# A selective scan with its row multiply moved to DVE and sums by identity matmuls, and an attention that normalises on GpSimd and transposes

## The chip, the cores and the metric

The kernel runs on one core of one Trainium2 chip. The engines are TensorE (PE for its matmuls, PEld for its weight loads), VectorE (DVE), ScalarE (ACT), GpSimd (POOL) and SyncE (SP), which here only starts DMAs. They run side by side and wait for each other through semaphores. The metric is the device time of one execution in microseconds (us); smaller is better. Everything is fp32.

## The reference

Eight images of 384 channels and 1024 positions pass a first layer (two Mamba scans, forward and backward, and a depthwise convolution), and then attention; five of the images have a feed-forward layer after it. What matters here, cut down:

```
def mamba(x, ...):
    ...
    delta = softplus(dt @ dt_proj_w.T + dt_proj_b)         # (b, l, 384)
    A = -exp(A_log)                                        # (384, 16)
    deltaA = exp(delta[..., None] * A)
    deltaBu = (delta * u)[..., None] * Bm[:, :, None, :]   # 16 states per channel
    def step(h, inp):
        dA, dBu, c = inp
        h = dA * h + dBu
        return h, einsum('bdn,bn->bd', h, c)               # summed over the 16 states
    _, ys = scan(step, h0, (deltaA, deltaBu, Cm))
    y = ys + u * D_param
    return (y * silu(z)) @ out_proj_w.T
...
scores = einsum('bhqd,bhkd->bhqk', q, k)                   # 6 heads, 1024 positions
attn = softmax(where(causal, scores, -inf))
out = einsum('bhqk,bhkd->bhqd', attn, v)
return out.reshape(B, T, 384) @ Wproj + bproj
```

## The kernel before, in words

Channels lie on partitions: 384 channels are NC = 3 chunks `c` of 128, and the 1024 positions lie along the free dimension, in NH = 2 halves of 512[...], or NT = 8 blocks of 128. The outer loop goes over the images b; one image runs `layer0`, `attention` and, for the first five, `feed_forward`.

In `layer0` the inputs are projected, convolved and passed through softplus into `u` (input), `dl` (delta) and `bcv` (the 16 B rows and 16 C rows, on 32 partitions), each for two directions d. L337 to L339 end the softplus, L370 turns `u` into `u*dl` on POOL. The two `bcv` go out to DRAM (L347).

The scan loops over d, over the n = 16 states and over the three chunks c:

- L377: a DMA reads a B row and a C row from DRAM and spreads each over 128 partitions (`brow`, `crow`; two buffers each).
- L385: POOL multiplies g = u*dl times brow, 128x1024, into one of six g buffers.
- L390: ACT makes the decays, da = exp(delta*A), 128x512, in PSUM.
- L396 (d = 0) or L399 (d = 1, reversed): DVE runs the recurrence over 512 positions, twice per c, the second half starting from the first one's last column.
- L402: POOL multiplies g by crow, in place.
- L404: PE adds eight transposes of g into `y` in PSUM, so that y gathers the sum over n and d with positions on partitions. L362 has put u times D there first.

After the scan ACT copies y to SBUF (L416), PE transposes it back (L424), DVE multiplies it by the gate `sz` (L428), and the output projection follows (L434, L441).

In `attention`, queries are worked on in blocks of 128: a head has two groups g of QT = 4 blocks. `probabilities` computes the scores of a block against the n = 128 to 1024 keys up to it (L502), adds the mask (L509), takes the row maximum (L513), the exponential with its row sum (L515) and the reciprocal (L516); L517 then makes on POOL a 128x128 diagonal matrix `dg` of the reciprocals. `weighted_values` turns every 128x128 block of probabilities by a matmul with dg as its moving operand (L529), which normalises it as well; DVE copies the result to SBUF (L537) and PE multiplies it by the values (L538). The loop calls `probabilities` of one group ahead of `weighted_values` of the group before it.

A framework inserts the semaphore waits and orders each engine's instructions by priority and its own estimate of times, so the order on an engine isn't that of the source; each engine then works through its queue in order. Buffers with the same tag are reused in turn: a write waits for the last reader of the buffer it takes.

Of the kernel before, what the change touches and what calls it, by code (L numbers as in the profile page):

```python
# [8 lines left out]
F32 = mybir.dt.float32  # L9
AF = mybir.ActivationFunctionType  # L10
ALU = mybir.AluOpType
AX = mybir.AxisListType
PSUM = bass.MemoryType.PSUM

P = 128
B, C, H, W = 8, 384, 32, 32
L = H * W
NC = C // P
HB = 512
NH = L // HB  # L20
NT = L // P
NS = 16
# [10 lines left out]
FFN_B = GROUPS * (B // GROUPS)  # L33
QT = HB // P
MASKED = -1e30
NR = 1


V_NORM, V_CW, V_CB, V_DTB, V_D, V_DW, V_DWB, V_BP, V_B2, V_ALOG = 0, 1, 5, 6, 7, 8, 17, 18, 19, 20
# [4 lines left out]
def kernel(  # L44
# [16 lines left out]
    nc = tc.nc  # L61
# [1 line left out]
    const = ctx.enter_context(tc.tile_pool(name="const", bufs=1))  # L63
    xpool = ctx.enter_context(tc.tile_pool(name="xpool", bufs=1))
    tpool = ctx.enter_context(tc.tile_pool(name="tpool", bufs=1))
    dpool = ctx.enter_context(tc.tile_pool(name="dpool", bufs=2, space=bass.MemoryType.DRAM))

    def ctile(name, shape):
        return const.tile(shape, F32, name=name, tag=name)
# [31 lines left out]
    ident = ctile("ident", [P, P])  # L101
# [9 lines left out]
    amat = ctile("amat", [P, NC, NS])  # L111
    nc.scalar.activation(amat, vec[:, :, V_ALOG : V_ALOG + NS], AF.Exp)
    nc.vector.tensor_scalar(amat, amat, -1.0, None, ALU.mult)
    diagd = ctile("diagd", [P, NC, P])
# [83 lines left out]
    def layer0(b, xt):  # L198
        t = tpool.tile([P, NC, L], F32, name=f"t_{b}", tag="t")
        with tc.tile_pool(name=f"l0_{b}", bufs=1) as lp:  # L200
# [140 lines left out]
                        )  # L341


            drows = []
            for d in range(2):
                dr = dpool.tile([2 * NS, L], F32, name=f"dr{d}_{b}", tag=f"dr{d}")
                nc.sync.dma_start(out=dr, in_=bcs[d])  # L347
                drows.append(dr)

            with tc.tile_pool(name=f"scan_{b}", bufs=2) as sp:
              with tc.tile_pool(
                name=f"yps_{b}", bufs=1, space=PSUM
              ) as yps, tc.tile_pool(name=f"scanps_{b}", bufs=2, space=PSUM) as ps:
                y = yps.tile([P, NC, NT, P], F32, name=f"y_{b}", tag="y")
                for d in range(2):
                    u, dl = us[d], dls[d]
                    for c in range(NC):  # L360
                        for j in range(NT):
                            nc.tensor.matmul(  # L362
                                out=y[:, c, j, :],
                                lhsT=u[:, c, j * P : (j + 1) * P],
                                rhs=diagd[:, c, :],
                                start=(d == 0 and j % 4 == 0),
                                stop=False,
                                skip_group_check=True,
                            )
                        nc.gpsimd.tensor_tensor(u[:, c, :], u[:, c, :], dl[:, c, :], ALU.mult)  # L370
                    for n in range(NS):
                        if n % NR == 0:
                            rows_bc = []
                            for which in range(2):
                                s = which * NS + n
                                rt = sp.tile([P, NR, L], F32, name=f"bc{which}_{d}_{b}_{n}", tag=f"bc{which}")
                                nc.sync.dma_start(  # L377
                                    out=rt,
                                    in_=drows[d][s : s + NR, :].unsqueeze(0).to_broadcast([P, NR, L]),
                                )  # L380
                                rows_bc.append(rt)
                        brow, crow = (rt[:, n % NR, :] for rt in rows_bc)
                        for c in range(NC):
                            g = sp.tile([P, L], F32, name=f"g_{d}_{b}_{n}_{c}", tag="g", bufs=6)
                            nc.gpsimd.tensor_tensor(g, u[:, c, :], brow, ALU.mult)  # L385
                            for i in range(NH):
                                h = i if d == 0 else NH - 1 - i
                                lo, hi = h * HB, (h + 1) * HB
                                da = ps.tile([P, HB], F32, name=f"da_{d}_{b}_{n}_{c}_{h}", tag="da")
                                nc.scalar.activation(  # L390
                                    da, dl[:, c, lo:hi], AF.Exp, scale=amat[:, c, n : n + 1]
                                )
                                gh = g[:, lo:hi]
                                if d == 0:
                                    first = 0.0 if i == 0 else g[:, lo - 1 : lo]
                                    nc.vector.tensor_tensor_scan(gh, da, gh, first, ALU.mult, ALU.add)  # L396
                                else:
                                    first = 0.0 if i == 0 else g[:, hi : hi + 1]
                                    nc.vector.tensor_tensor_scan(  # L399
                                        gh[:, ::-1], da[:, ::-1], gh[:, ::-1], first, ALU.mult, ALU.add  # L400
                                    )
                            nc.gpsimd.tensor_tensor(g, g, crow, ALU.mult)  # L402
                            for j in range(NT):
                                nc.tensor.matmul(  # L404
                                    out=y[:, c, j, :],
                                    lhsT=g[:, j * P : (j + 1) * P],
                                    rhs=ident,
                                    is_transpose=True,
                                    start=False,
                                    stop=(d == 1 and n == NS - 1),  # L410
                                    skip_group_check=True,
                                )

                yt = us[0].rearrange("p c (j k) -> p c j k", k=P)
                for c in range(NC):
                    nc.scalar.copy(yt[:, c], y[:, c])  # L416


              with tc.tile_pool(name=f"outps_{b}", bufs=8, space=PSUM) as ps:
                for c in range(NC):  # L420
                    for h in range(NH):
                        tp = ps.tile([P, HB], F32, name=f"yt_{b}_{c}_{h}", tag="mm")
                        for i in range(HB // P):
                            nc.tensor.transpose(  # L424
                                tp[:, i * P : (i + 1) * P], yt[:, c, h * (HB // P) + i, :], ident
                            )
                        gated = sz[:, c, h * HB : (h + 1) * HB]
                        nc.vector.tensor_tensor(gated, gated, tp, ALU.mult)  # L428
                for m in range(NC):
                    for h in range(NH):  # L430
                        cols = slice(h * HB, (h + 1) * HB)
                        op = ps.tile([P, HB], F32, name=f"op_{b}_{m}_{h}", tag="mm")
                        for c in range(NC):
                            nc.tensor.matmul(  # L434
                                out=op,
                                lhsT=wout[:, c, m * P : (m + 1) * P],
                                rhs=sz[:, c, cols],
                                start=(c == 0),
                                stop=(c == NC - 1),
                            )  # L440
                        nc.vector.scalar_tensor_tensor(  # L441
                            t[:, m, cols], op, rssm, t[:, m, cols], ALU.mult, ALU.add
                        )
# [3 lines left out]
    def attention(b, t):  # L447
        with tc.tile_pool(name=f"att_{b}", bufs=1) as ap, tc.tile_pool(
# [38 lines left out]
            with tc.tile_pool(name=f"attp_{b}", bufs=2) as pb, tc.tile_pool(  # L487
# [3 lines left out]
                def probabilities(hd, g):  # L491

                    c, r0 = hd // 2, (hd % 2) * HD
                    pr = pb.tile([P, QT, L], F32, name=f"pr_{b}_{hd}_{g}", tag="pr")
                    dg = pb.tile([P, QT, P], F32, name=f"dg_{b}_{hd}_{g}", tag="dg")
                    for i in range(QT):
                        qi = g * QT + i
                        n = (qi + 1) * P
# [15 lines left out]
                        rsum = small.tile([P, 1], F32, name=f"rsum_{b}_{hd}_{qi}", tag="rsum")  # L514
                        nc.scalar.activation(pr[:, i, :n], s[:, :n], AF.Exp, bias=nmax, accum_out=rsum)  # L515
                        nc.vector.reciprocal(rsum, rsum)  # L516
                        nc.gpsimd.tensor_scalar(dg[:, i, :], ident, rsum, None, ALU.mult)  # L517
                    return pr, dg

                def weighted_values(hd, g, pr, dg):  # L520
                    c, r0 = hd // 2, (hd % 2) * HD
                    av = ps.tile([P, HB], F32, name=f"av_{b}_{hd}_{g}", tag="av")
                    last = (g + 1) * QT - 1
                    for j in range(last + 1):
# [1 line left out]
                        cols = slice(i0 * P, HB)  # L526
                        pt = sps.tile([P, HB], F32, name=f"pt_{b}_{hd}_{g}_{j}", tag="pt")
                        for i in range(i0, QT):
                            nc.tensor.matmul(  # L529
                                out=pt[:, i * P : (i + 1) * P],  # L530
                                lhsT=pr[:, i, j * P : (j + 1) * P],
                                rhs=dg[:, i, :],
                                start=True,
                                stop=True,
                            )
                        ptn = small.tile([P, HB], F32, name=f"ptn_{b}_{hd}_{g}_{j}", tag="ptn")
                        nc.vector.tensor_copy(ptn[:, cols], pt[:, cols])  # L537
# [14 lines left out]
                waiting = None  # L552
                for hd in range(HEADS):
                    for g in range(NH):
                        made = (hd, g, *probabilities(hd, g))
                        if waiting is not None:
                            weighted_values(*waiting)
                        waiting = made
# [153 lines left out]
```

## Time and profile before

| what | value |
|---|---|
| median of 3 runs | 8059.35 us (8057.79 to 8061.69) |
| the profiled execution, its own time | 8061.69 us |
| its span from first to last instruction | 8059.7 us |
| mean granted TensorE clock | 0.721 |
| busy: PE, PEld | 5313.9 us, 3218.6 us |
| busy: DVE, ACT, POOL | 3689.0 us, 2388.8 us, 4230.6 us |
| image 0: scan stage | about 169 to 626 us |
| image 1: attention heads | about 1817 to 2007 us |

How to read the profile: the page has the busy time of each engine, the span in 40 slices with the busy share in tenths, and the costliest groups of instructions. A group's line has the line of the source, engine, operation, output and inputs, shapes and count; then busy us and mean ns of one; then the idle time of the engine ahead of these instructions and what ended it. A timeline line has start, duration, engine, line and shapes, and in brackets the idle time before it and the releaser. A duration counts from when the instruction is at the head of its engine, so one that is held back by something the semaphores don't show looks longer. A window table has, for a stretch of time, each engine's busy us and count, the granted clock, the DMA share and GB/s.

### The profile page before, as it was taken

How to read it: one execution, taken by the hardware profiler on the slowest of the kernel's cores; microseconds unless marked ns; L12 is line 12 of the kernel's file. 1: busy time of each engine (PE TensorE's matmuls, PEld its weight loads, DVE VectorE, ACT ScalarE, POOL GpSimd, SP SyncE). 2: the span in 40 equal slices, each digit the busy share in tenths (PEclk: the TensorE clock that was granted, in tenths of full speed). 3: DMA queues.
4: the chain of work that ended last, by engine and by line, in shares of the span. 5: the costliest groups of instructions: out<-in, count | busy, mean ns of one | idle time of the engine just before them, and what ended most of it. 6: DMA issues, size and time to landing. Idle time of an engine off the chain costs nothing. (4 is left out here: it accounts for less than half of the span.)

```text
span 8059.7 us, 53593 instructions
## 1 busy us (share of the span) xinstructions
PE 5313.9 (66%) x19274; PEld 3218.6 (40%) x19274; DVE 3689.0 (46%) x4109; ACT 2388.8 (30%) x3552; POOL 4230.6 (52%) x2163
## 2 busy tenths in 40 slices
PE   5447974469844599544997347974469544984469
PEld 2334533345423354233543334533345333543345
DVE  5554344534355533555334553344543555355533
ACT  4222224222242222422224222234222423233222
POOL 3992008951069810499101993108951499119951
PEclk7557985569965599755998557985569755985579
DMA  2220001210012100122000220001210122001200
GB/s 82 74 73 0 1 10 67 71 37 1 8 51 71 55 1 0 38 73 73 0 1 17 78 71 19 1 9 66 72 38 1 41 71 73 1 9 66 71 32 8
DMA packets 85838, 308.18 MB, mean 38 GB/s; under 512 B 9900, under 2 KB 12228, under 8 KB 85572
## 3 DMA queue, kind: packets, MB, share of 16 engines
q1 hardware_dynamic: 80896, 295.73, 10.6%
q10 hardware_dynamic: 4676, 9.03, 0.3%
q8 instruction: 151, 2.47, 0.1%
q14 instruction: 115, 0.94, 0.0%
HBM read 290.05 MB, written 14.68 MB: 38 GB/s over the span
## 5 line engine op out<-in xcount | busy, mean ns | idle before, releaser
L404 PE MATMUL y<-ident,g 128*128 128x128 f32 x6144 | 1507.1, 426 | 2262.5 <-POOL g L402 2262.5
L404 PEld LDWEIGHTS y<-ident,g 128*128 128x128 f32 x6144 | 1200.3, 222 | 2565.9 <-POOL g L402 2565.9
L390 ACT ACTIVATE da<-dl,amat 128x512 f32<-128x512 f32 x1536 | 1062.2, 692 | 2644.6 <-DVE g L396 1325.6
L385 POOL TENSOR_TENSOR g<-u,bc 128x1024 f32<-128x1024 f32 x768 | 1814.0, 2364 | 43.4 <-DMA bc<-dr 42.1
L402 POOL TENSOR_TENSOR g<-g,bc 128x1024 f32<-128x1024 f32 x768 | 1807.6, 2355 | 8.1 <-DVE g L396 4.2
L399 DVE TENSOR_TENSOR_SCAN g<-da,g 128x512 f32<-128x512 f32 x768 | 960.7, 1253 | 915.6 <-POOL g L385 874.2
L396 DVE TENSOR_TENSOR_SCAN g<-da,g 128x512 f32<-128x512 f32 x768 | 960.7, 1253 | 825.9 <-POOL g L385 784.7
L517 POOL TENSOR_SCALAR dg<-ident,rsum 128x128 f32<-128x128 f32 x384 | 231.7, 603 | 1769.8 <-DVE rsum L516 1767.3
L513 DVE TENSOR_REDUCE nm<-s 128x1 f32<-128x128 f32 (+7 forms) x384 | 290.3, 756 | 601.7 <-PE s L509 601.0
L515 ACT ACTIVATE pr<-s,nm 128x128 f32<-128x128 f32 (+7 forms) x384 | 284.2, 740 | 939.5 <-DVE nm L513 478.0
L220 POOL MEMSET xn<- 128x102 f32 (+1 forms) x32 | 5.6, 245 | 1003.7 <-DVE t L649 968.4
L537 DVE COPY ptn<-pt 128x512 f32<-128x512 f32 (+1 forms) x576 | 311.8, 555 | 474.7 <-PE pt L529 472.7
L502 PE MATMUL s<-k,q 64*128 64x512 f32 (+3 forms) x1152 | 502.6, 532 | 30.1 <-ACT pr L515 26.1
L529 PEld LDWEIGHTS pt<-dg,pr 128*128 128x128 f32 x3456 | 425.7, 192 | 210.6 <-issue 207.2
L529 PE MATMUL pt<-dg,pr 128*128 128x128 f32 x3456 | 498.5, 285 | 0.0
L538 PE MATMUL av<-ptn,v 128*64 128x512 f32 (+3 forms) x1152 | 464.1, 506 | 6.8 <-DVE ptn L537 6.4
L283 POOL TENSOR_TENSOR loc<-loc,xn 128x1024 f32<-128x1024 f32 x24 | 55.5, 2313 | 646.4 <-ACT loc L282 646.4
L635 PE MATMUL yp<-h,w2b 128*128 128x512 f32 x720 | 321.1, 609 | 27.7 <-ACT h L628 27.7
L615 PE MATMUL hp<-xf,w1b 128*128 128x512 f32 x720 | 312.4, 596 | 0.0
L320 PE MATMUL dp<-dt,wdt 24*128 24x512 f32 x192 | 129.4, 839 | 203.6 <-DVE dt L312 178.2
L467 PE MATMUL qp<-xa,wqkv 128*128 128x512 f32 x576 | 257.5, 609 | 0.0
L281 DVE SCALAR_TENSOR_TENSOR loc<-xn,vec,loc 128x1024 f32<-128x1024 f32 x192 | 250.4, 1346 | 2.8
(147 smaller groups left out, 5553.0 us busy)
## 6 DMA issues: line engine op xcount, KB each, us to landing
bc<-dr SPq DMA_DIRECT2D x512, 512.0 KB, 3.6
x<-in_x SPq DMA_DIRECT2D x8, 1536.0 KB, 6.4
out<-t SPq DMA_DIRECT2D x8, 1536.0 KB, 5.3
w1b<-in_w ACTq DMA_DIRECT2D x1, 2304.0 KB, 15.4
w2b<-in_w ACTq DMA_DIRECT2D x1, 2304.0 KB, 21.2
dr<-bcv SPq DMA_DIRECT2D x16, 128.0 KB, 1.9
wqkv<-in_w_qkv ACTq DMA_DIRECT2D x1, 1728.0 KB, 11.0
win<-in_w_in ACTq DMA_DIRECT2D x1, 1152.0 KB, 9.5
```

The costliest lines, as they stand in the source:

```text
L385: nc.gpsimd.tensor_tensor(g, u[:, c, :], brow, ALU.mult)
L390: nc.scalar.activation(da, dl[:, c, lo:hi], AF.Exp, scale=amat[:, c, n : n + 1])
L396: nc.vector.tensor_tensor_scan(gh, da, gh, first, ALU.mult, ALU.add)
L399: nc.vector.tensor_tensor_scan(gh[:, ::-1], da[:, ::-1], gh[:, ::-1], first, ALU.mult, ALU.add)
L402: nc.gpsimd.tensor_tensor(g, g, crow, ALU.mult)
L404: nc.tensor.matmul(out=y[:, c, j, :], lhsT=g[:, j * P : (j + 1) * P], rhs=ident, is_transpose=True, start=False, stop=(d == 1 and n == NS ...
L502: nc.tensor.matmul(out=s[:, k0:k1], lhsT=qk[0][r0 : r0 + HD, c, qi * P : n], rhs=qk[1][r0 : r0 + HD, c, k0:k1], start=True, stop=(k1 < n),)
L529: nc.tensor.matmul(out=pt[:, i * P : (i + 1) * P], lhsT=pr[:, i, j * P : (j + 1) * P], rhs=dg[:, i, :], start=True, stop=True,)
L537: nc.vector.tensor_copy(ptn[:, cols], pt[:, cols])
L538: nc.tensor.matmul(out=av[r0 : r0 + HD, cols], lhsT=v[:, j, hd * HD : (hd + 1) * HD], rhs=ptn[:, cols], start=(j == 0), stop=(j == last),)
L615: nc.tensor.matmul(out=hp, lhsT=w1b[:, c, m * P : (m + 1) * P], rhs=xn[:, c, cols], start=(c == 0), stop=(c == NC - 1),)
L635: nc.tensor.matmul(out=yp, lhsT=w2b[:, k, m * P : (m + 1) * P], rhs=hT[:, k, cols], start=(k == 0), stop=(k == NF - 1),)
```

## The change

Two parts of the kernel change at once.

In the scan, the B and C rows no longer pass through DRAM: PE spreads a row over the partitions by a matmul with a column of the identity (32 partitions in), and ACT copies it from PSUM to SBUF, two halves for each row. The decays da are one 128x1024 tile in SBUF in place of two 128x512 tiles in PSUM. The multiply by brow goes from POOL to DVE. The recurrence is one instruction over 1024. The g buffers are three, not six. y keeps channels on partitions: PE adds g by two matmuls of 512 columns with the identity, in place of eight transposes, and the copy and the transposes after the scan are gone; the output projection uses the scan's PSUM pool of two buffers, where it had one of eight.

In attention, POOL multiplies the whole row block of probabilities by the reciprocal in place, and PE turns the blocks by transposes; the diagonal matrix is gone.

```
-            drows = []
-            for d in range(2):
-                dr = dpool.tile([2 * NS, L], F32, ...)
-                nc.sync.dma_start(out=dr, in_=bcs[d])
...
-                y = yps.tile([P, NC, NT, P], F32, name=f"y_{b}", tag="y")
+                y = yps.tile([P, NC, NH, HB], F32, name=f"y_{b}", tag="y")
...
-                        for j in range(NT):
+                        for h in range(NH):
                             nc.tensor.matmul(
-                                out=y[:, c, j, :],
-                                lhsT=u[:, c, j * P : (j + 1) * P],
-                                rhs=diagd[:, c, :],
+                                out=y[:, c, h, :],
+                                lhsT=diagd[:, c, :],
+                                rhs=u[:, c, h * HB : (h + 1) * HB],
...
-                                rt = sp.tile([P, NR, L], F32, ..., tag=f"bc{which}")
-                                nc.sync.dma_start(
-                                    out=rt,
-                                    in_=drows[d][s : s + NR, :].unsqueeze(0).to_broadcast([P, NR, L]),
+                            row = sp.tile([P, L], F32, ..., tag=f"bc{which}")
+                            for h in range(NH):
+                                bp = ps.tile([P, HB], F32, ..., tag="mm")
+                                nc.tensor.matmul(
+                                    out=bp,
+                                    lhsT=ident[: 2 * NS, s : s + 1].to_broadcast([2 * NS, P]),
+                                    rhs=bcv[:, cols], ...
+                                nc.scalar.copy(row[:, cols], bp)
...
-                            g = sp.tile([P, L], F32, ..., tag="g", bufs=6)
-                            nc.gpsimd.tensor_tensor(g, u[:, c, :], brow, ALU.mult)
-                            for i in range(NH):
-                                ...
-                                da = ps.tile([P, HB], F32, ..., tag="da")
-                                nc.scalar.activation(da, dl[:, c, lo:hi], AF.Exp, ...)
-                                ...
-                                    nc.vector.tensor_tensor_scan(gh, da, gh, first, ALU.mult, ALU.add)
+                            da = sp.tile([P, L], F32, ..., tag="da")
+                            nc.scalar.activation(da, dl[:, c, :], AF.Exp, scale=amat[:, c, n : n + 1])
+                            g = sp.tile([P, L], F32, ..., tag="g", bufs=3)
+                            nc.vector.tensor_tensor(g, u[:, c, :], brow, ALU.mult)
+                            if d == 0:
+                                nc.vector.tensor_tensor_scan(g, da, g, 0.0, ALU.mult, ALU.add)
...
                             nc.gpsimd.tensor_tensor(g, g, crow, ALU.mult)
-                            for j in range(NT):
+                            for h in range(NH):
                                 nc.tensor.matmul(
-                                    out=y[:, c, j, :],
-                                    lhsT=g[:, j * P : (j + 1) * P],
-                                    rhs=ident,
-                                    is_transpose=True,
+                                    out=y[:, c, h, :],
+                                    lhsT=ident,
+                                    rhs=g[:, h * HB : (h + 1) * HB],
...
-                yt = us[0].rearrange("p c (j k) -> p c j k", k=P)
                 for c in range(NC):
-                    nc.scalar.copy(yt[:, c], y[:, c])
-              with tc.tile_pool(name=f"outps_{b}", bufs=8, space=PSUM) as ps:
-                            nc.tensor.transpose(tp[...], yt[:, c, ...], ident)
-                        nc.vector.tensor_tensor(gated, gated, tp, ALU.mult)
+                    nc.vector.tensor_tensor(sz[:, c, :], sz[:, c, :], y[:, c, :, :]..., ALU.mult)
...
-                        nc.gpsimd.tensor_scalar(dg[:, i, :], ident, rsum, None, ALU.mult)
-                    return pr, dg
+                        nc.gpsimd.tensor_scalar(pr[:, i, :n], pr[:, i, :n], rsum, 1.0, ALU.mult, ALU.mult)
+                    return pr
...
-                            nc.tensor.matmul(
-                                out=pt[:, i * P : (i + 1) * P],
-                                lhsT=pr[:, i, j * P : (j + 1) * P],
-                                rhs=dg[:, i, :],
+                            nc.tensor.transpose(
+                                pt[:, i * P : (i + 1) * P], pr[:, i, j * P : (j + 1) * P], ident
```

## The prediction

> **What bounds the kernel now.** I first read the page's busy shares and slices, then the costliest groups, then the waits and the order of time inside one scan. The slices repeat eight times, once per image:
>
> ```profile
> POOL 3992008951069810499101993108951499119951
> PEclk7557985569965599755998557985569755985579
> ```
>
> Where POOL stands at 9 to 10 tenths TensorE has half its clock: that is the scan. In the rest POOL is nearly idle and TensorE is at full clock. Two groups of the page fill POOL there:
>
> ```profile
> L385 POOL TENSOR_TENSOR g<-u,bc 128x1024 f32<-128x1024 f32 x768 | 1814.0, 2364 | 43.4 <-DMA bc<-dr 42.1
> L402 POOL TENSOR_TENSOR g<-g,bc 128x1024 f32<-128x1024 f32 x768 | 1807.6, 2355 | 8.1 <-DVE g L396 4.2
> L399 DVE TENSOR_TENSOR_SCAN g<-da,g 128x512 f32<-128x512 f32 x768 | 960.7, 1253 | 915.6 <-POOL g L385 874.2
> L529 PE MATMUL pt<-dg,pr 128*128 128x128 f32 x3456 | 498.5, 285 | 0.0
> ```
>
> Both multiplies have almost no idle time ahead of them, while the recurrence on DVE waited 874 us for POOL. The timeline gives the step, from one L385 start to the next:
>
> ```profile
> 604.06 2.41 POOL L385 TENSOR_TENSOR g<-u,bc 128x1024 f32<-128x1024 f32 x1
> 606.38 2.39 POOL L402 TENSOR_TENSOR g<-g,bc 128x1024 f32<-128x1024 f32 x1
> 606.50 2.61 DVE L399 TENSOR_TENSOR_SCAN g<-da,g 128x512 f32<-128x512 f32 x2 [2.00 <-POOL g L385]
> 608.68 2.40 POOL L385 TENSOR_TENSOR g<-u,bc 128x1024 f32<-128x1024 f32 x1
> ```
>
> So 4.615 us per (direction, n, c), 13.85 per n (three c). 256 such n make 3545 us of the 8059.7 us span. The DVE scan, which reads da from PSUM and g from SBUF, runs in 2.61 for two, fully beside POOL, and neither is stretched.
>
> Outside the scan the same two engines do collide, when a DVE instruction reads two SBUF tensors (timeline of the stage ahead of the scan):
>
> ```profile
> 149.69 2.33 POOL L370 TENSOR_TENSOR u<-u,dl 128x1024 f32<-128x1024 f32 x1
> 149.75 3.35 DVE L339 SCALAR_TENSOR_TENSOR dl<-dl,lw 128x1024 f32<-128x1024 f32 x1 [7.16 <-POOL lw L338]
> 151.99 3.32 POOL L338 TENSOR_TENSOR lw<-lw,w1m 128x1024 f32<-128x1024 f32 x1
> 155.27 2.78 POOL L370 TENSOR_TENSOR u<-u,dl 128x1024 f32<-128x1024 f32 x1
> 155.78 3.35 DVE L339 SCALAR_TENSOR_TENSOR dl<-dl,lw 128x1024 f32<-128x1024 f32 x1
> 163.78 1.23 DVE L339 SCALAR_TENSOR_TENSOR dl<-dl,lw 128x1024 f32<-128x1024 f32 x1 [4.65 <-POOL lw L338]
> ```
>
> Alone L339 takes 1.23 us. At 149.75 it takes 3.35: it ends at 153.10, 1.08 after POOL's L370 ends at 152.02. L338 started at 151.99 and ends at 155.31, 2.21 after that. They take turns, whole instructions at a time.
>
> In attention PE is the bound (window table of image 1: PE, PEld, DVE, ACT, POOL, clock):
>
> ```profile
> 1875.00:1885.00 10.00, 10.00 (x51) 5.68 (x49) 3.79 (x6) 0.00 (x0) 0.00 (x0) 1.00 0.01 2
> ```
>
> **What the skill says.** (1) The Trainium skill, "SBUF — State Buffer", Who interferes with whom: a DVE instruction with two SBUF inputs contends with a GpSimd instruction that reads SBUF, and the second one blocks until the first is done; with at most one SBUF input it doesn't. The trace agrees on both halves (3.35 against 1.23; 2.61 unstretched). (2) "DVE: opcode table, instruction layouts, handler registers and perf-mode slots", Datapath and trigger behaviour: the built-in tensor_tensor_scan runs at half throughput. The trace agrees: 1253 ns for 512 elements, where L339 takes 1.2 us for 1024. (3) "TensorE: Matmul & The Clock Gate", Part 1: the clock halves after an idle window of some 3.4 us and returns after a busy one. The trace agrees: 0.50 all through the scan, 1.00 some 4.5 us after the dense L424 begins.
>
> **The change, part by part: the scan.** Per n, the old step had six POOL multiplies. The new one has, on DVE, three multiplies T = u*brow and three scans S of 1024, all with two SBUF inputs (da now lies in SBUF), and on POOL three multiplies P by crow. By (1) each T or S excludes each P. Prices: P just after a DVE instruction adds 2.20 (above: 2.21); T just after a P adds 1.08; T after DVE work 1.20 - 0.07 = 1.13 (L268 lasts 1.28, but 18 in a row take 21.61 us, so each overlaps the next by some 0.07). S isn't in the trace at this size: the lower bound is two 512 rows' rate, 512 elements in 1253 ns less some 186 ns fixed, so 1024 take 2.13 + 0.15 = 2.28; the upper is 2 x 1253 = 2.51. I take 2.25 after DVE work and 2.15 after a P. In the built program's order DVE runs T0 S0 T1 T2 S1 S2. Taking turns, one n is S0 T1 T2 S1 P0 S2 P1 T0 P2: 3 x 2.20 + (2.15 + 2.15 + 1.08) + (1.13 + 1.13 + 2.25) = 16.49 us. Added plainly, without the overlap at the turn, 3 x (2.36 + 1.22 + 2.32) = 17.7: the upper bound.
>
> Is anything else later? ACT: three exponentials of some 1.1 (L331's rate) and four copies of 0.58 (L474): 5.6 of 16.5, hidden. DMA for the rows goes (SP had 512 issues; POOL waited 42 us for them in all, at the eight starts). PE: a 128x512 pass takes 0.43 at full clock (L434: 36 in 15.47) and 0.85 at half, and a plain fp32 matmul is two passes (18 calls there). Six y matmuls and four row spreads per n are 20 passes: 8.5 us at full, 17.1 at half clock. The queue on PE is y(n-1,2), crow(n), brow(n+1), y(n,0); P0(n) needs crow(n), and with three g buffers T2(n) needs y(n-1,2). At full clock crow is there 1.7 + 1.7 + 0.9 (copy and signals) = 4.3 us after P2, before its turn at 6.7: hidden. At half clock it comes at 7.7, after S2 has taken P0's turn; P0, P1, P2 then follow one another, the next T2 waits for the 10.2 us of y behind P0, and the cycle closes at 18.3 (17.1 of PE work and 1.2 of waiting). But then PE is 17 of 18.3 busy, y alone 10 us without a break, and by (3) the clock rises. I take a little of this slip: 16.8 per n. Gain or loss: (16.8 - 13.85) x 256 = +755 us. Bounds: 16.0 (+550) if turns overlap more, 18.3 (+1139).
>
> **Start, middle and end of each scan.** Start: the row DMA's 3.6 us goes, two copies and a multiply come. Middle: d=1 needs six y matmuls (about 8 us with the clock rising) and three POOL multiplies u*dl ahead of T0; before, the same place cost DVE 12.8 us. End: the ACT copies (2.84), 24 transposes (5.04) and their wait go, three DVE multiplies come, and the output projection then starts at half clock with two PSUM buffers in place of eight: about -4. I put the three together at 0, bounds -5 to +6 per image, -40 to +48.
>
> **Attention.** Turning a 128x128 block took two passes (x3456 for 1728 calls), a transpose takes one (L424: 24 calls an image, x192). L424 does 24 in 5.04 us at half clock, 0.2 each, so 0.107 at full, the rate of one pass of L529 (16 in 2.05). 1728 passes x 0.107 = -185 us where PE is the bound. Against it, POOL's step grows from 128 columns (603 ns) to 128..1024. Lower price: 1-input work at about line rate by "GPSIMD Engine Reference", Engine selection, estimated as 0.85 ns a column, so 1.4 us at 1024; upper: 603 ns a 128 columns, 4.8 us. Per head that is 8 to 22 us of the present 30.7 us (12 blocks an image; 11 take 168.8 us), so POOL doesn't bind, but the last block of a head reaches the transposes 0.8 to 4 us later, and PE's queue stands behind it. I take a loss of 1.8 us per head: -185 + 85 = -100, bounds -185 to +50.
>
> Sum: the profiled execution's own 8061.7 us (span 8059.7 and 2 around it; 2.3 above the median of the runs) + 755 + 0 - 100 = 8717, say 8715.
>
> **Rivals.** (a) PE stays at half clock, and its cycle of 18.3 sets the scan: 8062 + 1139 - 100 = 9100. For it: row spreads use 32 of 128 rows, and the K=24 matmul L320 kept the clock at 0.50 for ten dense us. Against: y fills more than the needed window. (b) The other side: S doesn't collide, since it takes its second input at half rate, and POOL works beneath it. Then DVE's 10.1 per n no longer counts; what is left is P2, y, crow, copy, three P: 4.3 + 6.9 = 11.2 at full clock, 14.6 at half. With 13, -218: 8062 - 218 - 100 = 7745. It decides from a lock time under 13.85 per n. Against it: L339 blocks for whole instructions, and nothing says that the slower read frees the port. (c) The lock holds, and attention loses: POOL at 4.8 us holds up PE, +150 in place of -100: 8965.
>
> **How the numbers follow.** Forecast 0.75, (a) 0.12, (b) 0.08, (c) 0.05. What a measurement can tell from no change is 0.2%, 16 us. Only (b) ends faster, mostly: faster 0.07, same 0.01, slower 0.92. Low end: 550 - 185 - 27 gives 8400. High end 9120 takes in (a) and (c).
>
> **What would show it.** In the profile after: S about 2.3 us when alone and near 4.5 when it meets P; P stretched by whatever is left of the T or S ahead of it; one n in 16.5 to 17 us; POOL and DVE together with hardly a gap; clock between 0.5 and 1. In attention, half as many L529 passes and an image's heads some 12 us shorter. It is wrong if S and P overlap unstretched, or if PE or ACT shows as what DVE waits for in the scan.

## The result, and the profile after

| | us, median | lowest to highest |
|---|---|---|
| before | 8058.57 | 8055.88 to 8061.69 |
| after | 8470.36 | 8458.24 to 8470.92 |

The changed kernel is slower: the ratio is 1.0507, with a 95% interval of 1.0489 to 1.0525, or +412 us. The forecast was 8715 us with a range of 8400 to 9120. The profiled execution took 8458.24 us (span 8456.5).

Before, the page had these slices for DVE:

```profile
DVE  5554344534355533555334553344543555355533
```

After, it has these:

```profile
DVE  6885448873378833688445985448873788458863
...
POOL 3663106651056610366202663106651466216641
...
PEclk7777987779977799777997778987779777987779
```

In the scan POOL was at 9 to 10 tenths and DVE at about 5. Now POOL is at 5 to 6, DVE at 8, and the TensorE clock is at 0.7 and not at 0.5. Neither engine is full by itself. The groups say how that can be:

```profile
L388 POOL TENSOR_TENSOR g<-g,bc 128x1024 f32<-128x1024 f32 x768 | 2858.1, 3745 | 1336.3 <-ACT bc L374 1264.1
...
L385 DVE TENSOR_TENSOR_SCAN g<-da,g 128x1024 f32<-128x1024 f32 x384 | 1393.2, 3654 | 4.4
...
L381 DVE TENSOR_TENSOR g<-u,bc 128x1024 f32<-128x1024 f32 x768 | 1012.5, 1344 | 503.1 <-PE y L390 396.0
...
L505 PE MATMUL pt<-ident,pr 128*128 128x128 f32 x1728 | 291.1, 285 | 0.0
```

The C multiply on POOL (L388) lasts 3745 ns where the same multiply took 2355 before, and the mean scan of 1024 lasts 3654 ns, though its shortest record is 2259. Both durations contain waiting for the other engine: a blocked instruction counts as busy. The idle column is therefore only part of the waits, and the 1264 us of POOL's wait for the copied C row (L374) is a suspect, not a proof. The order of time shows one n of image 0 (DVE and POOL only; the columns are start, length, engine, line, operation, tile, count, and in brackets the idle time ahead):

```profile
399.39 11.61 POOL L388 TENSOR_TENSOR g<-g,bc 128x1024 f32<-128x1024 f32 x3 [4.70 <-ACT bc L374]
...
407.39 1.41 DVE L381 TENSOR_TENSOR g<-u,bc 128x1024 f32<-128x1024 f32 x1 [1.82 <-PE y L390]
...
408.84 4.31 DVE L383 TENSOR_TENSOR_SCAN g<-da,g 128x1024 f32<-128x1024 f32 x1
...
413.07 2.33 DVE L381 TENSOR_TENSOR g<-u,bc 128x1024 f32<-128x1024 f32 x2
...
415.32 6.58 DVE L383 TENSOR_TENSOR_SCAN g<-da,g 128x1024 f32<-128x1024 f32 x2
...
415.70 8.34 POOL L388 TENSOR_TENSOR g<-g,bc 128x1024 f32<-128x1024 f32 x2 [4.70 <-ACT bc L374]
```

Read it as turns: T0 and S0, which is stretched to 4.31 by POOL's P2; T1 and T2 back to back in 2.33; S1 alone; S2 stretched by P0, together 6.58; then DVE idles 1.82 us under P1, and it begins again. This is the predicted order S0 T1 T2 S1 P0 S2 P1 T0 P2. Between two starts of POOL's groups, 399.39 and 415.70, lie 16.31 us for one n, where the kernel before took 13.85.

The stages of image 1, from starts of the same instructions in both traces:

| stage, us | before | after | difference |
|---|---|---|---|
| last softplus step to output projection (the scan) | 471.6 | 542.2 | +70.6 |
| first score to last attention copy (the heads) | 188.7 | 166.6 | -22.1 |

The same stages of all eight images, added up, make +567.6 for the scans and -182.9 for the heads, and the stretch between the two, from the output projection to the first score, makes +13.5. That is 398 of the 397 us between the two spans. Why that stretch is 1.7 us an image longer was not looked into. (In image 0 the heads are shorter by 27.6 us and not by 22.1. The profiled execution is 12 us faster than the median of 8470; part of that may lie there.)

### The profile page after: what moved, and what is told of

Read it like the earlier page. It is cut to its first block, busy times and chain, and to the rows that moved or that the text cites. A ratio compares the mean times of both kernels' runs of the same rounds, so it can differ in the third digit from the quotient of the medians.

```text
span 8456.5 us, 44878 instructions
## 1 busy us (share of the span) xinstructions
PE 6795.7 (80%) x15754; PEld 2798.8 (33%) x15754; DVE 5494.1 (65%) x4085; ACT 2690.4 (32%) x3768; POOL 3608.3 (43%) x1395
## 4 chain that ended last, share of the span: by engine, by line
PE 51%; POOL 23%; issue 12%; DVE 10%; ACT 4%; DMA 0%; POOLq 0%; ACTq 0%; DVEq 0%
POOL g L388 20%; PE y L390 12%; PE s L478 5%; PE bp L367 5%; PE av L510 5%; PE yp L607 4%; PE hp L587 4%; PE qp L444 3%; PE pt L505 3%; DVE loc L279 2%; DVE u L266 2%; ACT bc L374 2%; PE s L485 2%; PE ap L538 2%; PE vp L455 1%
## 5 line engine op out<-in xcount | busy, mean ns | idle before, releaser
L388 POOL TENSOR_TENSOR g<-g,bc 128x1024 f32<-128x1024 f32 x768 | 2858.1, 3745 | 1336.3 <-ACT bc L374 1264.1
L390 PE MATMUL y<-g,ident 128*128 128x512 f32 x3072 | 2209.7, 868 | 983.2 <-POOL g L388 982.8
L379 ACT ACTIVATE da<-dl,amat 128x1024 f32<-128x1024 f32 x768 | 880.9, 1148 | 2670.4 <-DVE g L385 1389.5
L390 PEld LDWEIGHTS y<-g,ident 128*128 128x128 f32 x3072 | 757.3, 268 | 2449.3 <-POOL g L388 1817.1
L385 DVE TENSOR_TENSOR_SCAN g<-da,g 128x1024 f32<-128x1024 f32 x384 | 1393.2, 3654 | 4.4
L383 DVE TENSOR_TENSOR_SCAN g<-da,g 128x1024 f32<-128x1024 f32 x384 | 1376.3, 3610 | 5.8
L381 DVE TENSOR_TENSOR g<-u,bc 128x1024 f32<-128x1024 f32 x768 | 1012.5, 1344 | 503.1 <-PE y L390 396.0
L367 PE MATMUL bp<-bcv,ident 32*128 32x512 f32 x2048 | 1050.2, 641 | 178.4 <-ACT bc L374 178.4
L374 ACT COPY bc<-bp 128x512 f32<-128x512 f32 x1024 | 567.0, 578 | 197.8 <-PE bp L367 94.5
L367 PEld LDWEIGHTS bp<-bcv,ident 32*128 32x128 f32 x2048 | 348.9, 190 | 847.5 <-ACT bc L374 506.8
L505 PE MATMUL pt<-ident,pr 128*128 128x128 f32 x1728 | 291.1, 285 | 0.0
```

The costliest lines, as they stand in the source:

```text
L367: nc.tensor.matmul(out=bp, lhsT=ident[: 2 * NS, s : s + 1].to_broadcast([2 * NS, P]), rhs=bcv[:, cols], start=True, stop=True,)
L374: nc.scalar.copy(row[:, cols], bp)
L379: nc.scalar.activation(da, dl[:, c, :], AF.Exp, scale=amat[:, c, n : n + 1])
L381: nc.vector.tensor_tensor(g, u[:, c, :], brow, ALU.mult)
L383: nc.vector.tensor_tensor_scan(g, da, g, 0.0, ALU.mult, ALU.add)
L385: nc.vector.tensor_tensor_scan(g[:, ::-1], da[:, ::-1], g[:, ::-1], 0.0, ALU.mult, ALU.add)
```

## The experiments

The theory: a DVE instruction with two SBUF inputs and a POOL multiply exclude each other, and the sum of their turns is the period of the new scan. The rivals: the spreading of rows over TensorE and ScalarE, TensorE's clock, or the three g buffers set it; or the scan, which runs at half rate, does not collide at all.

### Each part alone

`attn_only` is the kernel before with the attention lines of the diff; `scan_only` is the changed kernel with the old attention.

> The kernel before with the attention part of the change alone (probabilities multiplied in place, transposes), the scan as before. Stage times of the two traces say 22.1 us less per image in the heads, so -177: 7882 us. The prediction's own sum for this part was -100: 7958. The rival that GpSimd's longer step delays the heads by 150 us: 8208.

> The changed kernel with the old attention (diagonal matmuls): the scan part of the change alone. If the two parts only add, +70.6 us per image between the last softplus step and the output projection, so +565: 8624 us. The prediction's own sum for this part was +755: 8813. If the two parts help each other (a cooler TensorE, for one), the two single runs won't add up to the +412 of both.

Measured: `attn_only` 7889.21 us (ratio 0.9784, 0.9769 to 0.9798), -173 against its own runs of before at 8061.8. `scan_only` 8646.67 (1.0725, 1.0709 to 1.0741), +585. The two sum to +412, which is what both together gave. So the parts don't noticeably act on each other, and the stage times of image 1, taken eight times, gave both amounts within 20 us.

### Does the scan itself collide?

`before_da_sbuf`:

```diff
-                            g = sp.tile([P, L], F32, ..., tag="g", bufs=6)
+                            g = sp.tile([P, L], F32, ..., tag="g", bufs=5)
...
-                                da = ps.tile([P, HB], F32, ..., tag="da")
+                                da = sp.tile([P, HB], F32, ..., tag="da")
```

> The kernel before with one thing changed: the decays (two halves of 512) lie in SBUF, so that the scan reads two SBUF inputs (to make room, g has 5 buffers in place of 6). Theory (a VectorE instruction with two SBUF inputs and a GpSimd multiply take turns): GpSimd's two multiplies of 2.2 and the scan's two halves of about 1.15 no longer overlap, some 6.7 to 6.9 us per (d, n, c) in place of 4.615, 768 of them: +1600 to +1750, about 9650 to 9800 us. Rival (the scan doesn't collide, since it runs at half a multiply's rate): no change, 8058.

Measured: 9548.04 us, ratio 1.1842 (1.1822 to 1.1862), +1486. Its order of time in the scan:

```profile
605.44 2.34 POOL L402 TENSOR_TENSOR g<-g,bc 128x1024 f32<-128x1024 f32 x1
...
605.52 10.90 DVE L399 TENSOR_TENSOR_SCAN g<-da,g 128x512 f32<-128x512 f32 x4 [2.18 <-POOL g L385]
607.74 3.26 POOL L385 TENSOR_TENSOR g<-u,bc 128x1024 f32<-128x1024 f32 x1
...
612.23 3.11 POOL L402 TENSOR_TENSOR g<-g,bc 128x1024 f32<-128x1024 f32 x1 [1.23 <-DVE g L399]
...
615.30 3.26 POOL L385 TENSOR_TENSOR g<-u,bc 128x1024 f32<-128x1024 f32 x1
...
618.52 2.34 POOL L402 TENSOR_TENSOR g<-g,bc 128x1024 f32<-128x1024 f32 x1
```

From L402 at 605.44 to L402 at 618.52 two (d, n, c) pass: 6.54 us each, where it was 4.615. The surplus of 1.925 times 768 is 1478. The half scans, unstretched at 1253 ns with the decays in PSUM, now average 2.7 us, and POOL's multiplies reach 3.26. So the memory in which the decays lie is enough to make the scan collide; that the scan runs at half rate doesn't let POOL in. The 6.7 to 6.9 that were expected were 2 to 5% too high, since a half scan that follows a POOL multiply adds only some 1.07 us at the turn. This is the cleanest test of the mechanism: one buffer's memory and no other work differ, but for one g buffer less, and that isn't what POOL waits for (43.6 us of idle time ahead of L385 in the whole run, 42.4 of it for rows).

### What else could set 16.3 us?

`after_g4` gives the changed kernel a fourth g buffer; `after_rows_dma` takes the rows from DRAM by DMA, as the kernel before did (the lines that write them to DRAM are left out here):

```diff
-                            g = sp.tile([P, L], F32, ..., tag="g", bufs=3)
+                            g = sp.tile([P, L], F32, ..., tag="g", bufs=4)
```

```diff
-                            for h in range(NH):
-                                ...
-                                nc.tensor.matmul(out=bp, ...)
-                                nc.scalar.copy(row[:, cols], bp)
+                            nc.sync.dma_start(
+                                out=row, in_=drows[d][s : s + 1, :].to_broadcast([P, L])
+                            )
```

> The changed kernel with 4 g buffers in place of 3, so that the first B multiply of an n need not wait for y to have read the buffer (in the trace VectorE waits 1.5 to 1.9 us for that once per n). Theory (the turns of VectorE and GpSimd fill the period, the sum of the nine steps): no gain worth the name, 8430 to 8480 us. Rival (the buffer sets the period): 1.8 us less per n, 256 n, -460: about 8010.

> The changed kernel with the B and C rows spread by DMA again (as in the kernel before), so without the 4 spreading matmuls and 4 ScalarE copies per n; everything else as changed. Theory (turns of VectorE and GpSimd set 16.3 us per n): same, 8430 to 8500 us. Rival (TensorE's passes at a low clock, or the copied C row that GpSimd is shown to wait for, set the period): VectorE's 10.2 us per n or GpSimd's 7 would be the next bound, 1000 us or more faster.

Measured: `after_g4` 8524.33 us, `after_rows_dma` 8522.13, both some 50 us slower than the changed kernel's 8470 and just outside what was expected, on the side away from the rivals.

Rows by DMA: TensorE and ScalarE are lighter, POOL waits for no copy, and yet one n takes 16.36 us, from the first POOL multiply of one n to that of the next:

```profile
501.47 3.14 POOL L387 TENSOR_TENSOR g<-g,bc 128x1024 f32<-128x1024 f32 x1 [2.32 <-DVE g L384]
...
517.83 3.14 POOL L387 TENSOR_TENSOR g<-g,bc 128x1024 f32<-128x1024 f32 x1 [2.32 <-DVE g L384]
```

DVE's records between them leave hardly a gap (0.1 us in all), and in the whole run its B multiply idles 5.5 us for y to have read a buffer, where it was 396 in the changed kernel, with three g buffers in both. So neither the row spread nor the third buffer sets the period: the turns alone fill it. The profiled execution is 62 us slower all the same. The scan stages are 32 us of that (546.3 us in place of 542.2 in image 1, where the first multiply waits 4.04 us for the first row's DMA). The rest lies in the heads of images 0 and 1, 12 and 19 us longer, outside the scan; in image 1 TensorE's clock is 0.88 there (1932 to 2100 us), where it was 1.00.

The fourth buffer moved the waits in place of removing them. The page's groups of `after_g4`:

```profile
L388 POOL TENSOR_TENSOR g<-g,bc 128x1024 f32<-128x1024 f32 x768 | 2231.9, 2930 | 2031.6 <-ACT bc L374 1976.7
...
L381 DVE TENSOR_TENSOR g<-u,bc 128x1024 f32<-128x1024 f32 x768 | 1420.8, 1864 | 910.0 <-ACT bc L374 473.2
```

POOL is blocked less (2930 ns in place of 3745) but waits 1977 us for copied rows in place of 1264, and DVE waits for them too. From one group of POOL's multiplies to the next in its timeline (501.01 to 517.73) an n took 16.7 us. The wait for y hardly went (in image 1 DVE still idles 38.9 us for it, where it was 49.4), so this run is no clean test of the buffer; what it shows is that the copies on ScalarE now often come last. The row spread has next to no room left beneath the turns; in the changed kernel itself, the run with rows by DMA shows that it isn't what sets the period.

### Without a second engine: all on DVE

```diff
-                            nc.gpsimd.tensor_tensor(g, g, crow, ALU.mult)
+                            nc.vector.tensor_tensor(g, g, crow, ALU.mult)
```

> The changed kernel with the C multiply on VectorE too, so that no GpSimd instruction runs inside the scan. Theory (turns): every VectorE instruction runs at its own time, per n 3 x (1.13 + 2.28 + 1.13) = 13.6, with gaps up to 14.2, against 16.3: -540 to -690, about 7780 to 7930 us. Rival (no turns, something else sets 16.3 per n): moving work to VectorE can't help, 8470 or more. TensorE's 20 passes per n must run above a clock of 0.62 for the theory's time to show.

Measured: 7741.98 us, ratio 0.9611 (0.9597 to 0.9625) against before, so 728 us faster than the changed kernel by giving more work to the busier engine, and some 40 us below what was expected. Its order of time:

```profile
498.80 2.29 DVE L385 TENSOR_TENSOR_SCAN g<-da,g 128x1024 f32<-128x1024 f32 x1
...
501.00 1.20 DVE L381 TENSOR_TENSOR g<-u,bc 128x1024 f32<-128x1024 f32 x1
...
502.12 1.22 DVE L388 TENSOR_TENSOR g<-g,bc 128x1024 f32<-128x1024 f32 x1
...
503.25 2.28 DVE L385 TENSOR_TENSOR_SCAN g<-da,g 128x1024 f32<-128x1024 f32 x1
```

A scan adds 2.20 us, each multiply 1.12: 4.45 per (d, n, c), 13.35 per n. Nothing is stretched in these lines; over all scans the mean is 4.51. A product costs DVE half of what a turn of POOL takes from it, so in this scan POOL's help is worth less than nothing.

### Which products may go to which engine?

If only two-SBUF-input work collides, the best split keeps the decays in PSUM, leaves the C multiply on POOL beneath the scan, and moves only the B multiply. `t_on_dve` is the kernel before with one word changed, `t_on_dve_attn` adds the attention part:

```diff
-                            nc.gpsimd.tensor_tensor(g, u[:, c, :], brow, ALU.mult)
+                            nc.vector.tensor_tensor(g, u[:, c, :], brow, ALU.mult)
```

> The kernel before with only its B multiply moved from GpSimd to VectorE; decays stay in PSUM, rows by DMA, y by transposes. Theory: the scan (one PSUM input) runs beside GpSimd's C multiply, and only the B multiply must take its turn; if it starts right behind the scan ahead of on VectorE, before GpSimd's released multiply, a (d, n, c) takes 1.13 + 2.47 and gaps, 3.65 to 3.75 us in place of 4.615, -690: about 7370 us. Rival (GpSimd's multiply gets in first and VectorE waits it out): 2.2 + 1.1 + 2.47 = 5.8 per (d, n, c), +900: about 8960 us.

> The same with the attention part of the change: what the single edits promise in sum. Theory: the run without the attention part less 177 us, about 7190 us, which would beat both kernels. Rival (the attention part gains only beside the new scan): no faster than the run without it.

Measured: 8179.88 us (ratio 1.0152, 1.0137 to 1.0167) and 8004.39. The theory's number was missed by 800 us; that of its rival, 8960, by nearly as much. The order of time says why:

```profile
503.11 2.38 DVE L399 TENSOR_TENSOR_SCAN g<-da,g 128x512 f32<-128x512 f32 x2
...
504.55 2.34 POOL L402 TENSOR_TENSOR g<-g,bc 128x1024 f32<-128x1024 f32 x1 [2.44 <-DVE g L399]
505.42 2.56 DVE L385 TENSOR_TENSOR g<-u,bc 128x1024 f32<-128x1024 f32 x1
...
507.90 2.38 DVE L399 TENSOR_TENSOR_SCAN g<-da,g 128x512 f32<-128x512 f32 x2
```

The B multiply (L385) isn't queued behind a scan but between its two halves. The pair at 503.11 is the second half of one scan and the first of the next: the former ends at 504.30 and releases POOL, whose C multiply starts at 504.55. The B multiply comes at 505.42, waits the C multiply out and takes 2.56 in place of 1.2. So POOL does get in first, as the rival had it, but runs beneath a half scan for part of its time, and one (d, n, c) takes 4.79 and not 5.8. To test that, `t_order` changes only the place of this instruction in DVE's queue; `t_order_attn` adds the attention part:

```diff
-                            nc.vector.tensor_tensor(g, u[:, c, :], brow, ALU.mult)
+                            with tc.issue_after(last) if last is not None else nullcontext():
+                                nc.vector.tensor_tensor(g, u[:, c, :], brow, ALU.mult)
```

Here `last` is the second half of the scan before.

> As the kernel with only the B multiply moved to VectorE, and nothing else changed than its place in VectorE's queue: it is issued behind both halves of a scan, where it was issued between them. Theory: the multiply then starts at the moment at which GpSimd's C multiply is released, gets its turn first, and the C multiply runs beside the two scan halves that follow, so a (d, n, c) takes 1.13 + 2.38 and gaps, 3.55 to 3.75 us in place of the 4.79 of the run before: 7280 to 7450 us. Rival (GpSimd gets in first all the same): the C multiply's 2.2 us is waited out, 5.7 per (d, n, c), about 8900 us. Rival (the turns were never the cause, VectorE's own work is): no change, 8180.

> The same with the attention part of the change, whose gain was 170 to 176 us in the two runs before that had it alone: theory 7110 to 7280 us, faster than both kernels and than the version with all three products on VectorE (7742). Rival: if the order doesn't hold the turns, above 8000.

Measured: `t_order` 7485.04 us (ratio 0.9286, 0.9273 to 0.93), `t_order_attn` 7309.29 (0.9072, 0.9057 to 0.9087). The order of time of `t_order`:

```profile
501.51 1.20 DVE L387 TENSOR_TENSOR g<-u,bc 128x1024 f32<-128x1024 f32 x1
...
501.77 3.15 POOL L405 TENSOR_TENSOR g<-g,bc 128x1024 f32<-128x1024 f32 x1 [0.69 <-DVE g L401]
502.82 2.61 DVE L401 TENSOR_TENSOR_SCAN g<-da,g 128x512 f32<-128x512 f32 x2
...
505.35 1.20 DVE L387 TENSOR_TENSOR g<-u,bc 128x1024 f32<-128x1024 f32 x1
```

The B multiply starts first and keeps its 1.20; POOL's is stretched to 3.15, which costs nothing, and then runs beneath the scan. One (d, n, c) takes 3.84, a little over the 3.75 expected, and the 7485 us are 35 above the range: the scan now reads what the instruction just ahead of it wrote and starts 0.11 after that one's end, where in the run with all three products on DVE the records of neighbours overlap. The half scans agree with that: the two here, of which the second starts from the first one's last column, take 2.61, the two unrelated halves of `t_on_dve` 2.38. The same instructions in another order on one queue made 695 us of difference, and the result beats the kernel before by 752 us with the attention part.

### The attention part

Two things changed there, the kind of matmul and POOL's step. `attn_plain_mm` takes `attn_only` and turns with plain matmuls by the identity; `attn_pool_twice` repeats POOL's step:

```diff
-                            nc.tensor.transpose(
-                                pt[:, i * P : (i + 1) * P], pr[:, i, j * P : (j + 1) * P], ident
-                            )
+                            nc.tensor.matmul(out=pt[:, i * P : (i + 1) * P], lhsT=pr[:, i, ...], rhs=ident, ...)
```

```diff
                         nc.gpsimd.tensor_scalar(pr[:, i, :n], pr[:, i, :n], rsum, 1.0, ALU.mult, ALU.mult)
+                        nc.gpsimd.tensor_scalar(pr[:, i, :n], pr[:, i, :n], onecol, 1.0, ALU.mult, ALU.mult)
```

> As the run with the attention part alone, but the turning is done by plain matmuls with the identity in place of transposes (two passes each instead of one, 216 more per image). Theory (the part's gain is the passes it saves): 1728 passes of 0.107 us come back, +185: 8074 us, and the part without transposes is worth nothing. Rival (the gain comes from GpSimd's step or from building no diagonals): stays near 7889.

> As the run with the attention part alone, with GpSimd's in-place multiply followed by a second one of the same shape (by a column of ones): 384 more steps of 0.75 us on average, 286 us of GpSimd time. Theory (the step lies beside TensorE's work and only its first of a head could show): under +30, about 7890 to 7920 us. Rival (as the prediction charged it, the longer step delays the head's last group): 1.1 us for each of 96 groups or more, +85 to +290: 7975 to 8180.

Measured: `attn_plain_mm` 8061.12 us, ratio 1.0002 to before (0.9994 to 1.001): the whole gain is gone, and its page again counts the passes twice:

```profile
L528 PE MATMUL pt<-ident,pr 128*128 128x128 f32 x3456 | 498.3, 285 | 0.0
```

`attn_pool_twice` 7896.06 us, 7 more than `attn_only`. Its page:

```profile
L516 POOL TENSOR_SCALAR pr<-pr,rsum 128x128 f32<-128x128 f32 (+7 forms) x384 | 286.1, 746 | 1281.5 <-DVE rsum L515 1281.5
...
L517 POOL TENSOR_SCALAR pr<-pr,onecol 128x128 f32<-128x128 f32 (+7 forms) x384 | 286.8, 749 | 29.3
```

287 us more of POOL's work cost 7. The gain of the part is the passes saved, and POOL's step, however long within this bound, is hidden.

### The scans side by side

| us per (d, n, c) | B, C multiply | decays | from the timeline | (it - 4.615) x 768 | measured |
|---|---|---|---|---|---|
| before | POOL, POOL | PSUM | 4.615 | | |
| before_da_sbuf | POOL, POOL | SBUF | 6.54 | +1478 | +1486 |
| scan_only | DVE, POOL | SBUF | 5.44 | +634 | +585 |
| t_on_dve | DVE, POOL | PSUM | 4.79 | +134 | +122 |
| t_order | DVE first, POOL | PSUM | 3.84 | -595 | -576 |

(For `scan_only` the step is the changed kernel's 16.31 / 3; its measured time contains some -65 us at the ends of the scans.) Five arrangements of much the same arithmetic go by one rule: add up what can't run together, in the order in which it stands in the queues. It gives each measured time within 50 us.

## Why the prediction was right

The direction and the mechanism were right, and the time lay within the range, 245 us below the forecast: +657 us were forecast and +412 came. All its large misses are on one side, so nothing cancelled by luck. By its own steps, against the profiled 8458:

1. **The turns, 16.49 us per n.** Confirmed in order and nearly in size: the S that follows DVE work adds 2.20 (2.25 was taken), a P that follows an S some 2.15 (2.20 was taken), and an n takes 16.31, worth -46 us over 256 n. That two-SBUF-input scans collide was an inference from L339; moving only the decays showed it.
2. **The slip to 16.8 from TensorE's clock.** It did not come: windows of 20 us in image 1's scan show clocks of 0.68 to 0.90, and the period is that of the turns. The slip, 0.31 x 256, is -79 us. It was an addition for a case (the clock near a half) that the same paragraph argued against.
3. **Start, middle and end at 0.** They gave -8.1 us an image, -65 us, which is outside the bounds of -5 to +6 an image: 70.6 less the iterations' 2.46 x 32 = 78.7. Of this, some 6.3 lie at the end (last y to first projection 8.3 us before, 2.0 after), where -4 was seen and then rounded away, and some 2.9 at the start (last softplus step to the first multiply of the scan: 5.3 before, 2.4 after).
4. **Attention, -100.** The -185 for the passes was right: -177 by the stage times, -173 when made alone, +172 when the passes were put back. (Its check by L529, 16 records in 2.05 us, gives 0.128 a pass and not 0.107; the trace's saving over all heads, 182.9 us in 1728 passes, is 0.106.) The +85 against it was the mis-sized term, by two errors. The step was priced at up to 4.8 us for 1024 columns and took 1118 ns. And its lateness was charged once per head to TensorE, while doubling the step shows that TensorE hardly waits for it.

The four differences, -46, -79, -65 and -77, come to -267; the sum stood at 8717 and the profiled execution at 8458, 259 less. The stage times of all eight images put the third at -62 and the fourth at -83 and add the +13.5 between projection and scores, which no term of the prediction names; that makes -257. One sum of the prediction doesn't follow from its bounds: its low end of 8400 takes 27 us for start, middle and end, where its bound was 40, which makes 8387.

**A sign of being wrong that did appear.** The prediction would have been wrong "if PE or ACT shows as what DVE waits for in the scan". PE does show: DVE idles 396 us ahead of L381 until y has read a g buffer. But the 1.82 us of it in the n above lie under P1, whose turn T0 has to wait out anyway, and with rows by DMA that wait is gone and the period is still 16.36. The sign was badly chosen: a wait that lies beneath another engine's turn costs nothing.

**The rivals.** (a), TensorE at half clock: not seen, the clock rose, and without the row spread the period stayed. But the row spread is nearer to binding than the argument against it suggests: with a fourth g buffer the copied rows end most of POOL's waits and half of DVE's before its B multiply. (b), the scan doesn't collide: refuted by the one-buffer experiment, 1486 us. (c), attention loses: refuted.

**The pages it rested on.** What the Trainium skill, "SBUF — State Buffer", Who interferes with whom, states was borne out on each side: two SBUF inputs excluded POOL (6.54 us per step), one PSUM and one SBUF input did not (4.615). "GPSIMD Engine Reference", Engine selection, puts one-input work at roughly line rate; the measured slope, (1118 - 380) / 896 = 0.82 ns a column, agrees with the prediction's low price of 0.85, where its higher price, from scaling up the 128-column step, was too high by a factor of four.

## What to carry to other kernels

Count the SBUF inputs of each DVE instruction before moving work between DVE and POOL: in these runs those with two excluded POOL's multiplies, so that their times added, and a product done by POOL took twice as much from the pair as on DVE (2.20 us against 1.12). Where both engines are to be kept, put one input of the long DVE instruction in PSUM, and let the short one that must take a turn stand in the queue just where POOL is about to be released. In a trace, an instruction of DVE or POOL whose mean is far above its shortest record may be waiting while it counts as busy (here 3654 ns against 2259); look there before believing the idle column.

## What was not expected of the hardware

POOL's in-place multiply by two scalars takes 380 ns on 128 columns, 691 on 512 and 1118 on 1024. The old step, one scalar on 128 columns from the identity into another buffer, took 603. The by-form groups after:

```profile
L493 POOL TENSOR_SCALAR pr<-pr,rsum 128x1024 f32<-128x1024 f32 x48 | 53.6, 1118 | 70.5 <-DVE rsum L492 70.5
...
L493 POOL TENSOR_SCALAR pr<-pr,rsum 128x512 f32<-128x512 f32 x48 | 33.2, 691 | 67.6 <-DVE rsum L492 67.6
...
L493 POOL TENSOR_SCALAR pr<-pr,rsum 128x128 f32<-128x128 f32 x48 | 18.2, 380 | 654.0 <-DVE rsum L492 654.0
```

Whether the second operation, the buffer or the operand makes the difference was not tried.

The clock was another: TensorE's granted clock stood at 0.51 in the old scan and between 0.68 and 0.90 in the new one, and it did no good there, since TensorE was not what the period waited for.
